# Three hand-written lists of pieces laid out anew, and twelve products without a reader taken out

## The chip, the cores and the metric

One core of a Trainium2 chip runs the whole program. It has five engines with a list of instructions each: PE (matrix products), DVE and ACT (element-wise work), POOL (element-wise work and gathers) and SP (issues transfers). Each engine works through its list in order and waits on semaphores for the others. The metric is the device time of one execution in microseconds (us), lower is better; the figure of a kernel is the median of its runs.

## The reference

Every one of the 8192 tokens (16 sequences of 512, D = 512 features) gets six modulated copies of itself, a two-layer network over their concatenation, a layer norm and a residual:

```python
h = _ln(x, pw_g[pathway_ids], pw_b[pathway_ids])          # 500 rows to choose from
h = _ln(h, cp_g[compartment_ids], cp_b[compartment_ids])  # 5 rows
t = _ln(x, tm_g[time_steps], tm_b[time_steps])
m = x + _mlp_ln(memory_state, ...)[:, None, :]            # n, r alike, from the other states
s = _ln(x, ms_g[scale_type], ms_b[scale_type])
w = softmax(aw)
cat = concatenate([w[0]*h, w[1]*t, w[2]*m, w[3]*n, w[4]*r, w[5]*s], axis=-1)
y = silu(cat @ W1 + b1) @ W2 + b2                          # W1: 3072 x 512, W2: 512 x 512
return x + _ln(y, int_g, int_be)
```

## The kernel before

The branches t, m, n, r and s are linear in x or in the normalised x once the choice of rows is known, so the kernel sorts the tokens by that choice and folds the tables into weights. Three products of 512 x 512 are left for layer 1 of a token: X (the token itself times `wx_`), V (the normalised token times `vs`, a matrix per group of tokens, rebuilt on ACT and DVE when the group changes: pieces `sp` and `bd`, in an If) and H (the h branch times `wh_`). A row gathered per token (`add`) brings what does not depend on x.

The sorted tokens are worked on in 16 tiles of 512 tokens, each of four blocks of 128. Tiles overlap: while tile c is in layer 1, tile p = c-1 is in layer 2 and at its output, tile n = c+1 is being normalised and transposed, and tile m = c+2 is gathered.

The order of all work is written out by hand, in three lists of short names, called pieces. `ORDER` is the head (tables, the sort, all of tile 0 in layer 1 and the front of tile 1), `WINDOW` is run for tiles 0 to 14, and `LAST` for tile 15 and the end. A piece in a list issues its instructions on its engine when the list comes to it, so the list sets the order on each engine, and, for what one piece reads and another writes, who waits for whom. A name is a kind, a tile (a number, or p, c, n, m) and a block or half.

The pieces that this document speaks of:

- In the head: `ax` (PE turns `at_n`, L1025 and L980, for the gathers' index), `xt`, `xv`, `vt`, `vv` (PE transposes a block, ACT copies it into cX or cV, L1117 and L1123), `xs`, `xe`, `xm` (statistics of x), `wu` (`awake`, L401: products of a weight with itself into a bank whose result nobody reads).
- Layer 1: `lX`, `lV`, `lH` are eight products each of 512 columns (L392). From tile 1 on, X and H are done for pairs of blocks by seven half-size products instead of eight, `m7.c.half.1` to `.7` (L440), which accumulate into the banks `u_0`, `u_1` and `p1`. DVE makes their sums of tokens (`u1` to `u4`, L421 to L427) and adds `u` into the rows: `r1` (L449), `r2` (L451), `r5` (L453 and L454), `r3` (L457). `m7.c.0.6` goes into `u_0`, which `r5.c.0` reads.
- Between the layers: `ha`, `hs`, `tz` (add, silu, transpose on DVE and ACT), and `sZ`, `sH`, `sV`, `sX`: SP's transfers that spread the transposed blocks into cZ, cH, cV, cX (four of 64 KB each).
- Layer 2 in the same seven-product way: `q7.p.half.1` to `.7` (L541 and L543) into the banks `pq_0a`, `pq_0b`, `pq_1a`, `pq_1b`; POOL makes the sums (`zs`, L520 to L526). The banks are read by `kf` (ACT copies, L552 and L554), `ku` (ACT, L565), `sf` (DVE, L559 and L561) and `sl` (DVE, L570 and L572) into yb. `q7.p.1.5` and `q7.p.1.7` go into the two halves of `pq_1b`; `kf.p.3` reads the first half, `sf.p.3` the second.
- The end of a tile: `lv`, `lp`, `lb` (L629 and L630) and `po` (POOL scatters the output, L634). The front of the next: `tv` (DVE transposes xm, L190), `f1` (L335 and L336), `f2`, `fv` (L357), `th`.
- In `LAST`: `l2` is the plain layer 2 of tile 15, `la`, `yg`, `ft` (L603, L580, L599) its end on DVE.

Of the kernel before, what the change touches and what calls it, by code (L numbers as in the profile page):

```python
# [44 lines left out]


WINDOW = """
    ha.p.2 lV.c.1 hs.p.2 sh.c.1 tz.p.3 gc.c.2 tz.p.2 sp.c.3 gc.c.3 f1.c.2 fs.c.2 f1.c.3 m7.c.1.1 m7.c.0.1 lV.c.0
    xs.n.0 fs.c.3 sh.c.0 bd.c.3 lV.c.3 fv.c.2 f2.c.2 f2.c.3 sZ.p.2 ga.c.0 sZ.p.0 xs.n.1 q7.p.1.1 fp.c.2 fv.c.3 fn.c.2
    q7.p.0.1 sZ.p.1 fp.c.3 q7.p.0.2 fn.c.3 sZ.p.3 sp.c.2 th.c.2 th.c.3 xs.n.2 zs.p.0 zs.p.1 bd.c.2 q7.p.0.5 kf.p.0  # L50
    q7.p.1.2 sH.c.0 sf.p.0 gh.n.0 zs.p.2 tx.n.3 kf.p.1 tx.n.0 q7.p.0.6 xs.n.3 zs.p.4 q7.p.0.7 ku.p.0 zs.p.5 q7.p.1.5
    zs.p.3 xe.n kf.p.2 tx.n.1 xp.n ga.c.1 sf.p.1 sH.c.3 tx.n.2 xm.n kf.p.3 q7.p.0.3 q7.p.1.7 sf.p.2 nv.n.3 q7.p.0.4
    sl.p.0 zs.p.6 nv.n.1 ga.c.2 zs.p.7 sh.c.3 tv.n.3 tv.n.1 r1.c.0 gc.n.0 sf.p.3 sl.p.1 nv.n.2 tv.n.2 m7.c.0.2 nv.n.0
    ga.c.3 sH.c.2 sH.c.1 lq.p.0 gh.n.1 tv.n.0 q7.p.1.3 lq.p.1 q7.p.1.6 ku.p.1 f1.n.0 q7.p.1.4 sl.p.2 fs.n.0 sl.p.3
    lV.c.2 lq.p.2 u1.c.0 u1.c.1 lq.p.3 va.n u3.c.0 sV.n.0 sV.n.3 u2.c.0 lv.p m7.c.0.4 r1.c.1 m7.c.0.5 lp.p m7.c.1.5
    u2.c.1 fv.n.0 lb.p.1 lb.p.0 vd.n r5.c.0 gc.n.1 u4.c.0 m7.c.0.6 u3.c.1 r5.c.1 gx.m.1 lb.p.2 sp.n.1 po.p.0 r2.c.0
    sV.n.2 f1.n.1 fp.n.0 m7.c.1.6 sV.n.1 sX.n.2 sX.n.0 m7.c.0.7 gx.m.2 sX.n.3 fs.n.1 sp.n.0 r2.c.1 f2.n.0 lb.p.3
    po.p.1 fv.n.1 gx.m.0 gx.m.3 fn.n.0 po.p.2 fp.n.1 bd.n.0 bd.n.1 f2.n.1 m7.c.1.7 m7.c.1.2 fn.n.1 u4.c.1 m7.c.0.3
    r3.c.0 th.n.0 gh.n.2 sh.c.2 ha.c.0 ha.c.1 r3.c.1 hs.c.1 m7.c.1.4 th.n.1 gh.n.3 hs.c.0 tz.c.1 ha.c.3 hs.c.3 po.p.3
    tz.c.0 sX.n.1 m7.c.1.3  # L60
"""
# [15 lines left out]


# [1402 lines left out]
```

## Time and profile before

| | |
|---|---|
| median of 3 runs | 938.56 us (936.71 to 940.25) |
| profiled execution, its span | 935.9 us |
| PE busy | 909.9 us, 97% of the span |
| DVE busy | 745.0 us, 80% |
| POOL busy | 655.0 us, 70% |
| ACT busy | 502.1 us, 54% |

The profile is of one execution. Its time is the span, 935.9 us, and what lies around it; against the median of the runs 2.7 us lie around it. Rows of instructions give the start, the duration, engine, line, operation, the tile written and read, the shapes and a count, and in brackets how long the engine was idle before and what ended that. A duration holds the latency of the pipeline, so instructions on one engine overlap in the rows; from start to start is what one costs the engine.

### The profile page before, as it was taken

How to read it: one execution, taken by the hardware profiler on the slowest of the kernel's cores; microseconds unless marked ns; L12 is line 12 of the kernel's file. 1: busy time of each engine (PE TensorE's matmuls, PEld its weight loads, DVE VectorE, ACT ScalarE, POOL GpSimd, SP SyncE). 2: the span in 40 equal slices, each digit the busy share in tenths (PEclk: the TensorE clock that was granted, in tenths of full speed). 3: DMA queues.
4: the chain of work that ended last, by engine and by line, in shares of the span. 5: the costliest groups of instructions: out<-in, count | busy, mean ns of one | idle time of the engine just before them, and what ended most of it. 6: DMA issues, size and time to landing. Idle time of an engine off the chain costs nothing. (4 is left out here: it accounts for less than half of the span.)

```text
span 935.9 us, 13631 instructions
## 1 busy us (share of the span) xinstructions
PE 909.9 (97%) x3711; PEld 649.5 (69%) x3711; DVE 745.0 (80%) x1359; ACT 502.1 (54%) x1211; POOL 655.0 (70%) x705
## 2 busy tenths in 40 slices
...
GB/s 277 256 183 192 181 226 196 185 238 167 247 170 237 189 209 208 194 207 201 237 181 250 165 240 176 219 208 209 204 195 214 201 234 164 247 166 180 185 46 99
DMA packets 88861, 186.68 MB, mean 199 GB/s; under 512 B 24372, under 2 KB 24372, under 8 KB 88780
## 3 DMA queue, kind: packets, MB, share of 16 engines
...
q14 instruction: 50, 0.41, 0.1%
q10 hardware_dynamic: 704, 0.08, 0.1%
...
## 5 line engine op out<-in xcount | busy, mean ns | idle before, releaser
L392 PE MATMUL p<-vs,cV 128*128 128x512 f32 x504 | 226.3, 596 | 4.0 <-ACTq L237 2.3
L392 PEld LDWEIGHTS p<-vs,cV 128*128 128x128 f32 x504 | 95.9, 191 | 108.5 <-issue 89.5
L339 ACT ACTIVATE junk<-pw 128x512 bf16<-128x512 f32 x60 | 37.7, 629 | 175.2 <-DVE pw L336 84.9
L440 PE MATMUL p<-wh__80,cH 128*128 128x256 f32 x480 | 111.1, 379 | 0.0
L164 POOL DMA_INDIRECT xbs<-in_x,tok x64 | 69.2, 1081 | 44.4 <-DVE yb L630 24.7
L440 PEld LDWEIGHTS p<-wh__80,cH 128*128 128x128 f32 x480 | 91.2, 190 | 12.4
L634 POOL DMA_INDIRECT out<-yb,tok x64 | 65.4, 1023 | 41.8 <-issue 29.2
L164 POOL DMA_INDIRECT pw<-in_pw,i_pw x64 | 64.7, 1010 | 39.0 <-DVE rH L190 19.9
L164 POOL DMA_INDIRECT cp<-cp_rows,i_cp x64 | 78.8, 1231 | 17.5 <-issue 12.2
L380 POOL TENSOR_TENSOR xbs<-xbs,rows 128x512 f32<-128x512 f32 x64 | 82.2, 1286 | 1.2
L164 POOL DMA_INDIRECT add<-rows,i_add x64 | 67.0, 1048 | 14.7 <-issue 12.5
L361 POOL TENSOR_TENSOR rsh<-veh,mhalf 128x1 f32<-128x1 f32 x64 | 49.2, 768 | 37.2 <-DVE veh L357 32.4
L365 ACT ACTIVATE pw<-pw,rsh 128x512 f32<-128x512 f32 x64 | 44.8, 717 | 53.8 <-issue 23.7
L463 ACT ACTIVATE add<-add 128x512 f32<-128x512 f32 x64 | 38.5, 626 | 63.8 <-DVE add L460 45.4
L335 DVE SCALAR_TENSOR_TENSOR pw<-xbs,sums,pw 128x512 f32<-128x512 f32 x60 | 53.6, 893 | 18.5 <-DMA pw<-in_pw,i_pw 16.2
L372 DVE SCALAR_TENSOR_TENSOR pw<-pw,sumsh,cp 128x512 f32<-128x512 f32 x60 | 44.5, 748 | 18.7 <-DMA cp<-cp_rows,i_cp 7.8
L190 DVE STREAM_TRANSPOSE rH<-pw 128x512 f32<-128x512 f32 x60 | 41.3, 703 | 20.5 <-ACT pw L365 19.8
L440 PE MATMUL p<-wt,cH 128*128 128x256 f32 x240 | 56.7, 379 | 0.0
L440 PE MATMUL u<-wt,ss 128*128 128x256 f32 x240 | 54.5, 380 | 0.4 <-DVE add L454 0.4
L440 PE MATMUL u<-wt,cX 128*128 128x256 f32 x240 | 54.4, 380 | 0.0
L440 PEld LDWEIGHTS u<-wx__79,cX 128*128 128x128 f32 x240 | 45.6, 190 | 12.6 <-issue 5.0
L440 PE MATMUL u<-wx__79,cX 128*128 128x256 f32 x240 | 54.2, 379 | 0.0
...
## 6 DMA issues: line engine op xcount, KB each, us to landing
cZ<-rZ SPq DMA_DIRECT2D x256, 64.0 KB
...
```

The source lines that it names most:

```text
L164: nc.gpsimd.indirect_dma_start(dst, None, table, bass.IndirectOffsetOnAxis(ap=idx, axis=0), **kw)
L190: nc.vector.transpose(rot[:, :, :, j, :].rearrange("p q c t -> p c q t"), src.rearrange("p (c q t) -> p c q t", c=NC, q=Q))
L335: nc.vector.scalar_tensor_tensor(h, st["xb"][:, j, :], st["sums"][:, 1, j : j + 1], h, ALU.add, ALU.mult)
L339: nc.scalar.activation(junk, x, AF.Identity, accum_out=sums[:, 0, k : k + 1])
L361: nc.gpsimd.tensor_tensor(rs, st.pop(("ve", j)), mhalf[:, :1], ALU.pow)
L365: nc.scalar.mul(pw[:, :D], pw[:, :D], st.pop(("rs", j)))
L372: nc.vector.scalar_tensor_tensor(pw[:, :D], pw[:, :D], st["sh", j][:, 1], cp, ALU.add, ALU.mult)
L380: nc.gpsimd.tensor_add(st["xb"][:, j, :], st["xb"][:, j, :], rows[:, 2, :])
L392: nc.tensor.matmul(st["p1", g], st["c" + blk][:, g, c, :], m[:, c, :], start=(blk == first and c == 0), stop=(blk == last and c == NC - 1) ...
L440: nc.tensor.matmul(dst, m[:, c], at_["half1"][k][:, c], start=(k == 1 and c == 0), stop=(c == NC - 1), skip_group_check=True)
L463: nc.scalar.activation(st["add", g], st["add", g], AF.Silu)
L634: nc.gpsimd.indirect_dma_start(out_rows[j], bass.IndirectOffsetOnAxis(ap=tok[:, j, w : w + 1], axis=0), yb[:, j, :], None)
```

## The change

The text of the three lists is new, and nothing else. From `ORDER` the twelve `wu` pieces are gone; the function `awake` stays, without a caller. All other pieces are the same, in another order: on every engine in the head, in the steady groups and in the last group.

```diff
 ORDER = """
-    wk.1.2 h2.1 fx dk lt pk bx sz wk.1.1 by kd wu.lX.0.1.0 xs.0.0 xt.0.0 tk tt wk.1.3 wk.2.1 gx.e0.0 xv.0.0
-    wu.lX.0.1.8 lw fg lo xs.0.1 fl.2 wm.4 h2.2 gx.e0.1 wu.lX.0.1.1 fl.1 scl he.1 xt.0.1 ax he.2 gx.e0.3 gx.e0.2 ac
...
+    se lw lo lt wk.1.0 wk.1.2 fx bx dk wk.1.3 wk.1.1 wk.2.1 by kd tk fg h2.1 ax cv xt.0.1 xv.0.1 he.1 fl.2 tt
+    xs.0.1 pwi gx.e0.0 gh.0.2 gx.e0.1 gh.0.0 xs.0.3 xs.0.2 xs.0.0 xe.0 wk.2.2 xp.0 xt.0.0 h2.2 h2.0 cg xm.0 he.0
...
 WINDOW = """
...
-    zs.p.3 xe.n kf.p.2 tx.n.1 xp.n ga.c.1 sf.p.1 sH.c.3 tx.n.2 xm.n kf.p.3 q7.p.0.3 q7.p.1.7 sf.p.2 nv.n.3 q7.p.0.4
...
+    sl.p.0 nv.n.3 kf.p.3 nv.n.1 q7.p.1.7 q7.p.0.4 zs.p.7 tv.n.3 sf.p.3 tv.n.1 sl.p.1 sH.c.0 sH.c.2 sH.c.1 sH.c.3
+    q7.p.1.6 q7.p.1.4 q7.p.1.3 lV.c.2 nv.n.2 nv.n.0 lq.p.0 ku.p.1 f1.n.0 sl.p.2 tv.n.2 sl.p.3 f1.n.1 lq.p.1 fs.n.0
```

What stands on the engines at three places. A row is a line, an operation, the tile written and read with its number, the shape, and a count where it repeats.

The first is PE in the head, around the transposes of `ax` (tile `pa`). Before:

```order
L401 MATMUL awake_lX_0_1_563<-wt_82 128x512
L1117 MATMUL ptX1_635<-ident_93,xbs2_90 128x128 x4
L1025 MATMUL pa_640<-ident_93,room1_115 128x64
L980 MATMUL pa_640<-at_n_285,ident_93 32x16 x16
L1129 MATMUL po0_681<-xbs1_89,room1_115 32x512 x4
L1099 MATMUL pdr_686<-tg_122,picks_199 34x512
L401 MATMUL awake_ex_4_688<-wt_82 128x512
```

Now:

```order
L1048 MATMUL pnx_520<-b_at_290,room1_115 64x7 x4
L1048 MATMUL pnx_520<-b_at_290,g_at_291 64x7 x8
L1129 MATMUL po1_558<-xbs0_88,room1_115 32x512 x4
L1025 MATMUL pa_563<-ident_93,room1_115 128x64
L980 MATMUL pa_563<-at_n_285,ident_93 32x16 x16
L1188 MATMUL pv_581<-ident_93,vr_278 128x9 x4
L1117 MATMUL ptX1_586<-ident_93,xbs2_90 128x128 x4
```

The products into `awake` are gone, and `pa` stands ahead of the transposes of x (`ptX`), behind the first `po`.

The second is PE in a steady group, in layer 2 of tile 5, around the bank `pq5_1b`. Before:

```order
L541 LDWEIGHTS ident_93
L541 MATMUL pq5_1b_3794<-b2r_104,ident_93 128x256
L543 MATMUL pq5_1b_3794<-w2_81,cZ5_3779 128x256 x2
L543 MATMUL pq5_0b_3804<-w2_81,yb_91 128x256 x2
L543 MATMUL pq5_1b_3794<-w2t_1432,zs5_3862 128x256 x2
L543 MATMUL pq5_0b_3804<-w2t_1432,cZ5_3779 128x256 x2
L440 MATMUL p1_6_0_3751<-wh__80,cH6_3844 128x256 x4
L543 MATMUL pq5_1b_3794<-w2_81,zs5_3862 128x256 x2
```

Now:

```order
L543 MATMUL pq5_0b_3782<-w2_81,yb_91 128x256 x2
L541 LDWEIGHTS ident_93
L541 MATMUL pq5_1b_3849<-b2r_104,ident_93 128x256
L543 MATMUL pq5_1b_3849<-w2_81,cZ5_3772 128x256 x2
L543 MATMUL pq5_1b_3849<-w2t_1407,zs5_3863 128x256 x2
L543 MATMUL pq5_0b_3782<-w2t_1407,cZ5_3772 128x256 x2
L543 MATMUL pq5_1a_3848<-w2t_1407,zs5_3863 128x256 x2
L543 MATMUL pq5_1b_3849<-w2t_1407,cZ5_3772 128x256 x2
```

The product into `pq5_0b` that stood between the first two products into `pq5_1b` now stands ahead of both.

The third is DVE in the same group, from the front of tile 6 to `r5` of tile 5. The first part, before:

```order
L335 SCALAR_TENSOR_TENSOR pw6_0_3412<-xbs2_90,sums_3318,pw6_0_3412 128x512
L336 SCALAR_TENSOR_TENSOR pw6_0_3412<-pw6_0_3412,rsx_3438 128x512
L570 TENSOR_TENSOR yb_91<-yb_91 128x256
L572 TENSOR_TENSOR yb_91<-yb_91,pq4_1b_3356 128x512
L237 UNCONDITIONAL_BRANCH
L421 TENSOR_TENSOR ss5_3522<-cX5_3179,cH5_3406 128x512 x2
L425 TENSOR_TENSOR cX5_3179<-cX5_3179 128x512
L423 TENSOR_TENSOR ss5_3522<-ss5_3522,cX5_3179 128x512
L616 TENSOR_SCALAR vey_3546<-ssy_3495 128x4
L449 TENSOR_TENSOR add5_2_3464<-add5_2_3464,u5_1_3303 128x256
L423 TENSOR_TENSOR ss5_3522<-ss5_3522,cX5_3179 128x512
```

Now:

```order
L190 STREAM_TRANSPOSE rV6_3463<-xm6_2_3496 128x4x4x32
L572 TENSOR_TENSOR yb_91<-yb_91,pq4_1b_3411 128x512
L335 SCALAR_TENSOR_TENSOR pw6_1_3435<-xbs2_90,sums_3288,pw6_1_3435 128x512
L336 SCALAR_TENSOR_TENSOR pw6_1_3435<-pw6_1_3435,rsx_3433 128x512
L237 UNCONDITIONAL_BRANCH
L421 TENSOR_TENSOR ss5_3526<-cX5_3244,cH5_3468 128x512 x2
L616 TENSOR_SCALAR vey_3529<-ssy_3500 128x4
L190 STREAM_TRANSPOSE rV6_3463<-xm6_0_3498 128x4x4x32
L423 TENSOR_TENSOR ss5_3526<-ss5_3526,cX5_3244 128x512
L449 TENSOR_TENSOR add5_2_3547<-add5_2_3547,u5_1_3302 128x256
L357 TENSOR_SCALAR veh_3558<-sumsh_3511 128x1
L427 TENSOR_TENSOR cH5_3468<-cH5_3468,ss5_3526 128x512
```

The second pair of `f1` (tile `pw6_1`) now stands ahead of the sums of tokens, and a transpose of `xm6` and the sum into cH (L427) among them. The end of the stretch, before:

```order
L629 SCALAR_TENSOR_TENSOR yb_91<-yb_91,rsy_3557,rows_92 128x512
L630 TENSOR_TENSOR yb_91<-yb_91,xbs0_88 128x512
L228 TENSOR_LOAD new_v_106
L453 TENSOR_TENSOR add5_0_3346<-add5_0_3346,u5_0_3308 128x256
L454 TENSOR_TENSOR add5_1_3440<-add5_1_3440,u5_0_3308 128x256
L427 TENSOR_TENSOR cH5_3406<-cH5_3406,ss5_3522 128x512
L425 TENSOR_TENSOR cX5_3179<-cX5_3179 128x512
```

Now:

```order
L629 SCALAR_TENSOR_TENSOR yb_91<-yb_91,rsy_3553,rows_92 128x512
L630 TENSOR_TENSOR yb_91<-yb_91,xbs0_88 128x512
L425 TENSOR_TENSOR cX5_3244<-cX5_3244 128x512
L453 TENSOR_TENSOR add5_2_3547<-add5_2_3547,u5_1_3302 128x256
L454 TENSOR_TENSOR add5_3_3551<-add5_3_3551,u5_1_3302 128x256
L453 TENSOR_TENSOR add5_0_3330<-add5_0_3330,u5_0_3312 128x256
L454 TENSOR_TENSOR add5_1_3555<-add5_1_3555,u5_0_3312 128x256
```

The pair that adds `u5_1` stood behind the pair that adds `u5_0` and the sums of tokens after it, and now stands ahead of that pair; a sum of tokens (L425) that stood further up now follows the two `lb`.

More of the change, by code (lines that the diff above doesn't have):

```diff
@@ new lines @@
+    f2.0.2 cn fl.1 cw ct vt.0.3 xt.0.3 vt.0.2 fl.0 ca wk.2.0 cm xs.e0.3 fn.0.2 xe.e0 pk gr.e0.1 xp.e0 xm.e0 nv.0.0
+    nv.e0.1 vv.0.3 scl ht.0.2 vt.0.0 f2.0.0 mt.e0.1 wk.2.3 cr gx.e1.2 gr.e0.0 ey.1 gh.0.1 rp.0 xs.e1.1 xv.0.3
+    xv.0.2 va.1 nv.e0.0 nv.e0.3 xs.e1.0 vv.0.0 lX.0.1 fv.0.0 ar mt.e0.0 f1.0.1 fs.0.1 xa ey.0 rp.1 fp.0.0 gx.1.0
+    gc.0.1 gx.1.3 fn.0.0 ez.0 nv.e0.2 rc.0 xs.e1.2 wl.4 rc.1 sp.0.1 vv.0.2 ez.1 ro.0 ro.1 ht.0.0 ex.0 lX.0.2
+    lX.0.3 f2.0.1 bd.0.1 hv.0.0 fv.0.1 xe.e1 gx.1.2 gr.e0.2 gr.e0.3 ea.0 gh.0.3 gx.1.1 xp.e1 mt.e0.2 mt.e0.3 ee.0
@@ new lines @@
+    xm.e1 vd.0 ey.2 ey.3 gc.0.3 gr.e1.2 fp.0.1 xs.1.2 xs.1.3 wh sp.0.0 va.0 ez.3 nv.e1.2 xs.1.0 fn.0.1 xs.1.1 ez.2
+    eo.0 f1.0.3 fs.0.3 mt.e1.2 tx.1.0 f2.0.3 fv.0.3 hv.0.2 tx.1.2 xe.1 ex.1 lV.0.1 ey.6 lX.0.0 ht.0.1 sh.0.2 ea.3
+    ea.2 ea.1 fp.0.3 gr.e1.0 xp.1 gh.1.3 fn.0.3 ez.6 wm.0 sp.0.3 nv.e1.0 wm.1 nv.e1.1 wm.2 ht.0.3 ex.3 gr.e1.1
+    gh.1.2 ea.6 bd.0.0 tx.1.3 bd.0.3 hv.0.1 mt.e1.1 xm.1 mt.e1.0 ee.3 tx.1.1 ee.1 lV.0.0 ex.6 ey.4 ey.5 wm.3 ez.5
+    nv.1.1 sp.0.2 ez.4 nv.1.2 wl.1 f1.1.3 bd.0.2 tv.1.1 ee.6 f1.1.2 eo.3 eo.1 eo.6 ex.2 ex.5 ex.4 lV.0.2 lV.0.3
@@ new lines @@
+    gc.1.2 gc.1.3 ea.4 ea.5 sp.1.0 fs.1.3 nv.1.3 sp.1.1 fs.1.2 ee.5 ee.2 vd.1 tv.1.3 bd.1.0 hv.0.3 fv.1.3 fv.1.2
+    f2.1.3 f2.1.2 fp.1.3 fp.1.2 nv.1.0 fn.1.3 wl.0 wl.2 fn.1.2 wl.3 bd.1.1 ee.4 th.1.3 th.1.2 wq tv.1.2 tv.1.0
+    gc.1.0 sh.0.0 gh.1.1 gh.1.0 eo.5 eo.2 lH.0.0 lH.0.3 sX.1.0 gc.1.1 sp.1.3 gx.2.0 eo.4 wb lH.0.2 f1.1.0 f1.1.1
+    lH.0.1 sX.1.3 sX.1.1 sX.1.2 sV.1.1 sV.1.3 sV.1.0 sV.1.2 ga.0.2 gx.2.1 ga.0.0 ga.0.3 ga.0.1 sh.0.3 sh.1.1
+    ha.0.0 ha.0.2 ha.0.3 fs.1.0 fs.1.1 hs.0.2 hs.0.0 sp.1.2 hs.0.3 bd.1.3 tz.0.2 bd.1.2 tz.0.3 fv.1.0 fv.1.1
@@ L56 @@
[L56 to L60, printed above, removed]
+    ha.p.2 lV.c.1 gc.c.2 gc.c.3 f1.c.2 tz.p.3 sp.c.3 hs.p.2 tz.p.2 fs.c.2 xs.n.0 f1.c.3 fv.c.2 f2.c.2 bd.c.3
@@ new lines @@
+    bd.c.3 fv.c.3 bd.c.2 f2.c.3 f2.c.2 sZ.p.1 sZ.p.0 m7.c.1.1 lV.c.3 lV.c.2 m7.c.0.1 q7.p.0.1 fp.c.2 fp.c.3 ga.c.3
+    ga.c.2 zs.p.0 zs.p.1 zs.p.2 zs.p.3 ga.c.0 fn.c.3 fn.c.2 kf.p.0 th.c.3 th.c.2 q7.p.0.5 q7.p.0.6 q7.p.0.7 kf.p.1
+    ku.p.0 sH.c.2 sH.c.0 sH.c.1 sH.c.3 sZ.p.3 sZ.p.2 sf.p.1 q7.p.0.2 q7.p.0.4 m7.c.1.2 q7.p.0.3 m7.c.0.2 m7.c.0.4
+    sl.p.0 r1.c.0 sf.p.0 sl.p.1 r1.c.1 u1.c.0 u2.c.0 u1.c.1 lq.p.0 lq.p.1 u2.c.1 u4.c.0 vr.p.1 u3.c.1 u3.c.0
+    vr.p.0 u4.c.1 m7.c.0.5 m7.c.1.5 m7.c.1.6 m7.c.0.6 m7.c.1.3 pr.p.1 ga.c.1 pr.p.0 zs.p.4 zs.p.5 sh.c.0 zs.p.6
```

61 lines of the change are left out of this document (22 added, 39 removed).

## Prediction

> **What bounds the kernel now.** I read the busy shares first, then the stretches, then the chain of PE's waits, last the order of time on PE and DVE inside one steady group.
>
> ```profile
> PE 909.9 (97%) x3711; PEld 649.5 (69%) x3711; DVE 745.0 (80%) x1359; ACT 502.1 (54%) x1211; POOL 655.0 (70%) x705
> ```
>
> PE is the bound: 97% busy, DVE 80%. The table of stretches (length, busy time of PE, PEld, DVE, ACT, POOL, then the granted clock) says where PE's few idle microseconds lie: in the head, and not in a steady group.
>
> ```profile
> 37.23:47.47 10.24, 10.24 (x56) 6.22 (x55) 7.56 (x28) 2.24 (x10) 4.27 (x5) 0.50 0.68 232
> 47.47:80.07 32.60, 29.76 (x186) 12.39 (x186) 18.00 (x57) 20.82 (x48) 19.24 (x19) 1.00 0.56 186
> 80.07:143.24 63.17, 61.59 (x161) 27.95 (x159) 48.24 (x89) 44.25 (x94) 43.42 (x43) 1.00 0.69 203
> ...
> 146.46:149.87 3.41, 3.41 (x5) 1.35 (x4) 1.05 (x2) 0.00 (x0) 2.64 (x4) 0.50 0.95 266
> ```
> ```profile
> 303.17:353.79 50.62, 50.62 (x206) 38.07 (x205) 40.40 (x73) 26.75 (x66) 37.71 (x38) 1.00 0.74 206
> 710.78:762.49 51.71, 50.92 (x206) 37.98 (x205) 44.21 (x78) 29.65 (x71) 37.89 (x40) 1.00 0.72 203
> 151.32:814.26 662.94, 660.05 (x2654) 493.50 (x2653) 550.37 (x974) 361.37 (x879) 489.28 (x489) 1.00 0.73 206
> ```
>
> A steady group takes 50.62 us, and PE works through all of it; DVE has 10 us to spare over the group, but that average says nothing about one place in the list. From the same product of one group to that of the next, 13 groups take 662.94 us, 4.9 over 13 x 50.62; the group of 710.78 alone has 1.1 of that (PE idle 0.8), and in all 13 PE is idle for 2.9. PE's waits, in total, number and longest:
>
> ```profile
> PE p L392 <- ACTq L237: 2.3, 1, 2.3
> ...
> PE pq_0a L543 <- DVE yb L559: 1.0, 1, 1.0
> ...
> PE pq_1b L543 <- DVE yb L561: 0.7, 1, 0.7
> PE pq_0b L543 <- POOL cZ L522: 0.4, 1, 0.4
> ...
> PE u L440 <- DVE add L454: 0.4, 1, 0.4
> ```
>
> So whatever order is better can win a few microseconds in the steady groups, and whatever order is worse is paid 14 times.
>
> **The head.** Removed: the 12 products without a reader. They stand on PE, but what counts is what stood behind them: `ax`, PE's transposes for the index of the gathers, is now the fourth piece. ACT's waits up to the last copy into cX, which the first product of layer 1 (80.07 us) needs:
>
> ```profile
> 54.64 0.21 ACT L1039 COPY at_n<-pa 128x64 f32<-128x64 f32 x1 [4.11 <-PE awake_ex L401]
> ...
> 66.55 0.81 ACT L306 ACTIVATE xm<-xbs,nmx,rsx 128x512 f32<-128x512 f32 x1 [2.40 <-issue]
> 70.10 0.59 ACT L1227 COPY br<-pb 128x512 f32<-128x512 f32 x1 [2.74 <-PE pb L1222]
> ...
> 76.49 0.59 ACT L1258 COPY rows<-pr 120x512 f32<-120x512 f32 x1 [1.84 <-DVE six L1003]
> ...
> 78.55 0.61 ACT L1123 COPY cX<-ptX 128x512 f32<-128x512 f32 x1
> ```
>
> The four waits sum to 11.1 us: the most that can be won ahead of that copy; the least is nothing, if other waits take their place. I take 7, nearer the upper end, since the 4.11 goes for certain and pieces that ACT needs (xm, f1) move ahead of what it waits for. Layer 1 of tile 0 is then 63.17 us of nearly full PE, the same products; of the 7 I let 2 be lost to gathers on POOL, whose list has no idle to give. At 143.24 PE waited 2.3 us for ACT's branch at L237, which stood behind a silu; the branch (`sp.1.2`) now comes two pieces earlier, and with the wait goes the half clock of 146.46 to 149.87, worth half of 3.41, 1.7. Together 7 - 2 + 2.3 + 1.7 = 9 us won, between 2 and 13.
>
> [...] By the clock of 1.00 that the rows give for the stretches after 47.47, I leave the sum at -9.
>
> **Steady group, first place: q7 into pq_1b.** In the order before, another product (q7.0.3, into pq_0b) stood between q7.1.5 and q7.1.7. Now these two are neighbours. q7.1.7 writes the bank from which ACT copies the result of q7.1.5 (L554), and waits for that copy. PE and ACT in the group of 249 us, then the same three in the last group, where before, too, the copy ended last:
>
> ```profile
> 269.46 1.10 PE L543 MATMUL pq_1b<-w,cZ 128*128 128x256 f32 x4
> 270.40 1.03 PE L543 MATMUL pq_0b<-w,yb 128*128 128x256 f32 x4
> 271.27 1.03 PE L543 MATMUL pq_1b<-w2t,zs 128*128 128x256 f32 x4
> 272.13 1.03 PE L543 MATMUL pq_0b<-w2t,cZ 128*128 128x256 f32 x4
> ...
> 277.31 3.60 PE L392 MATMUL p<-vs,cV 128*128 128x512 f32 x8
> ...
> 285.92 1.24 PE L440 MATMUL u<-wt,ss 128*128 128x256 f32 x5
> ```
> ```profile
> 270.65 0.37 ACT L554 COPY yb<-pq_1b 128x256 f32<-128x256 f32 x1 [1.17 <-POOL rsx L289]
> ```
> ```profile
> 908.73 1.13 PE L543 MATMUL pq_1b<-w,cZ 128*128 128x256 f32 x4 [0.44 <-POOL cZ L522]
> ...
> 910.23 0.37 ACT L554 COPY yb<-pq_1b 128x256 f32<-128x256 f32 x1 [1.63 <-PE pq_1b L543]
> ...
> 910.65 0.73 PEld L543 LDWEIGHTS pq_1b<-w2t,zs 128*128 128x128 f32 x4 [0.33 <-ACT yb L554]
> 910.65 1.13 PE L543 MATMUL pq_1b<-w2t,zs 128*128 128x256 f32 x4
> ```
>
> Issue of q7.1.5 ends at 270.40, the copy ends at 271.02: with nothing between, PE stalls 271.02 - 270.40 = 0.62 and a little for the signal. In the last group the stretch from the four products' end (908.73 + 0.97 = 909.70) to q7.1.7 is 0.95. I take 0.65, with 0.95 as upper end; the lower is 0, if PE doesn't wait for a copy of the other half of the bank. [...]
>
> **Steady group, second place: r5 ahead of m7.0.6.** m7.0.6 writes u_0 and waits until DVE's r5.0 (L453, L454) has read it. DVE's list from sf.3, which needs q7.1.7, to the end of r5.0, in the group of before:
>
> ```profile
> 273.41 0.41 DVE L561 TENSOR_TENSOR yb<-yb,pq_1b 128x256 f32<-128x256 f32 x1
> ...
> 274.34 1.29 DVE L190 STREAM_TRANSPOSE rV<-xm 128x512 f32<-128x512 f32 x2
> 275.55 0.71 DVE L335 SCALAR_TENSOR_TENSOR pw<-xbs,sums,pw 128x512 f32<-128x512 f32 x1
> ...
> 277.05 0.43 DVE L570 TENSOR_TENSOR yb<-yb 128x256 f32<-128x256 f32 x1
> ...
> 281.92 0.75 DVE L629 SCALAR_TENSOR_TENSOR yb<-yb,rsy,rows 128x512 f32<-128x512 f32 x1 [0.18 <-POOL rsy L621]
> ...
> 284.71 0.41 DVE L453 TENSOR_TENSOR add<-add,u 128x256 f32<-128x256 f32 x1
> ...
> 285.37 0.68 DVE L427 TENSOR_TENSOR cH<-cH,ss 128x512 f32<-128x512 f32 x1
> 285.97 0.68 DVE L425 TENSOR_TENSOR cX<-cX 128x512 f32<-128x512 f32 x1
> ```
>
> Before: 285.37 - 273.41 = 11.96, of which 0.18 a wait, so 11.78 of work, and PE's m7.0.6 (285.92) came 0.55 later: no stall. Now the same stretch also holds, start to start, f1.n.1 (277.05 - 275.55 = 1.50), a third transpose tv (0.60), u4.1 (285.97 - 285.37 = 0.60) and r5.1 (0.66, as r5.0): 15.14. sf.3 can't begin before q7.1.7 is done, 0.27 after its issue (the row of 271.27: 1.03 long, next issue after 0.86; 0.1 for the signal). On PE, from the end of issue of q7.1.7 to m7.0.6, stand the same pieces in number: four q7, one lV, four m7, 285.92 - 272.13 = 13.79. Stall: 0.27 + 15.14 - 13.79 = 1.62, whatever slack DVE brought into the group, since both ends of the chain hang on q7.1.7. I take 1.65; it could be 1.0 if DVE's operations run shorter beside less traffic, and 2.2 if a wait (a root, a copy) falls into the chain. What is queued behind r5.0 on DVE (u3.1, lb.1, r2.0) is late by as much, but its readers (m7.0.7) have three PE pieces of 1.73 before them.
>
> The group becomes 50.62 + 0.65 + 1.65 = 52.9. Fourteen of them cost 32 us (14 x 1.4 = 20 to 14 x 3.15 = 44). The later PE also hides some of the 4.9 us above 13 x 50.62: -3 (0 to -5).
>
> **Costed at nothing.** SP's spreads: sZ.p.0 and 1 now go first, which is what q7.0 needs first; sH and sV come later by at most one spread set, behind PE's older work. POOL: sh.c.3 and the gathers for two groups on end its list; it is busy 37.7 of 50.62, and if its cover went, each shift would cost about 1.3. ACT's nv.n.3 ahead of the copy: its input is there before.
>
> **The end.** DVE's chain behind the last product of layer 2 took, before:
>
> ```profile
> 928.18 0.69 DVE L603 TENSOR_TENSOR yb<-p,rows 128x512 f32<-128x512 f32 x1
> ...
> 930.24 0.75 DVE L599 SCALAR_TENSOR_TENSOR yb<-yg,sd,xbs 128x512 f32<-128x512 f32 x1
> ```
>
> 2.81 us; now two blocks' scale and sum stand behind it, some 1.7 more (two operations of 0.61 and 0.66, and a root). The last group's waits above (0.7, 0.4 and their like on pq_1b) mostly go: 1.5 back. Net 0, within 1.5.
>
> **Sum.** Profiled execution 935.9; -9 + 32 - 3 + 0 gives 955.9. The median of the runs, 938.56, is 2.7 above it: 958.6, so 958.
>
> **Rivals.**
> 1. *Neither steady wait is real* (DVE reaches r5.0 in time, the copy doesn't hold q7.1.7); then only the head shows: 938.6 - 9 = 930 (926 to 936), faster. For it: DVE has 10 us spare per group and before had no stall at either place. Against: the chain hangs on q7.1.7 at both ends, so spare time elsewhere can't be spent in it. It decides if the chain is under 13.5 us.
> 2. *One of the two:* 14 x 0.65 or 14 x 1.65 alone, less 9 and 3: 936 to 950.
> 3. *Cold head.* Without the twelve products PE stays at 0.50 in the sparse head. Priced by the half clock of 146.46: layer 1's opening costs 1.7 to 3.4 more and the transposes ahead of it 2 to 3: +5, with both waits 963. That clock of 1.00 after 47.47 came with the products, so the trace can't exclude it. [...]
> 4. *The reorder does nothing:* steady groups at 50.6 and ACT's head waits replaced by others: 936 to 941.
>
> **Chances.** Both waits with a warm head 0.54, with a cold head 0.18, one wait 0.13, rival 1 0.10, rival 4 0.05. Likeliest: 958, its own range 947 to 967. The range 932 to 968 leaves out most of rival 1 and the tails. 0.5% is 4.7 us, about what these runs (936.71 to 940.25) can tell from no change: faster 0.12 (rival 1 and an end of rival 2), same 0.08, slower 0.80.
>
> **What would show it.** After: a steady period of 52.9 on PE; among PE's waits, `u L440 <- DVE add L454` some 14 times at 1.6 and `pq_1b L543 <- ACT yb L554` some 14 times at 0.65; no L401 rows; the first layer 1 product near 73; no 0.50 clock near 140. A period of 50.6 with neither wait makes the prediction wrong; so does a new wait elsewhere, a product that waits for a spread above all.

## Result and the profile after

The changed kernel is slower by 12%: 1050.39 us (1048.23 to 1055.6, 4 runs) against 937.63 us (935.19 to 940.25, 4 runs) beside it, a ratio of 1.1196 with a 95% interval of 1.1154 to 1.1238. The forecast was 958, with a range of 932 to 968: the sign was right, the size was not. The profiled execution has a span of 1046.4 us, 110.5 more than before. Its busy shares, in the order of the page (busy time, share, instructions):

```profile
PE 937.7 (90%) x3687; PEld 663.5 (63%) x3687; DVE 740.4 (71%) x1359; ACT 499.0 (48%) x1211; POOL 648.6 (62%) x705
```

PE, with its weight loads (PEld), is the only engine with more busy time (909.9 and 649.5 before), although it has 24 instructions fewer: some of its work ran at half clock (0.50 in the last row below). The stretches (length, busy time of PE, PEld, DVE, ACT, POOL, granted clock, share of the DMA engines, GB/s): a whole steady group of the changed kernel, and the piece of it behind its longest wait.

```profile
438.84:498.67 59.83, 54.61 (x205) 39.91 (x204) 41.16 (x74) 26.62 (x66) 37.75 (x39) 0.94 0.62 176
...
478.26:484.49 6.23, 6.22 (x15) 4.97 (x16) 3.17 (x6) 0.72 (x1) 3.95 (x6) 0.50 0.30 106
```

The 205 products that took 50.62 us of a full PE now take 59.83: 5.2 us idle, and 54.61 busy instead of 50.62. The period, here and below the mean distance from the first product into `pq_0a` of one group to that of the next over 13 groups, is 59.01 (51.00 before). PE's waits after:

```profile
PE u L440 <- DVE add L454: 47.7, 14, 4.7
PE p L440 <- DVE cH L427: 16.5, 14, 1.2
...
PE pq_1b L543 <- issue: 5.9, 7, 1.2
PE p L392 <- DVEq L237: 3.8, 1, 3.8
PE pq_1b L543 <- ACT yb L554: 3.7, 5, 1.2
PE pq_1b L543 <- POOL cZ L522: 2.4, 2, 2.2
```

The two waits of the prediction are there, `u L440 <- DVE add L454` in 14 groups and `pq_1b` (put down to the copy, to issue or to others) in about as many. The second has the forecast size or somewhat more, 0.5 to 1.2 in most groups; the first is 3.31 in 13 groups, and 4.65 in the last, where 1.62 was forecast. A third wait, for cH, was not forecast at all. By parts of the span: the first product into u of tile 1 comes at 144.80 instead of 151.32, 6.5 us earlier; between tile 1 and the start of the last group the 14 groups lose 114.6; the last group and the end take 2.4 more.

Why 3.31: DVE and PE in the group at 456 us, in order of time (start, duration, then the instruction, in brackets the idle time before and what ended it).

```profile
459.56 0.42 DVE L561 TENSOR_TENSOR yb<-yb,pq_1b 128x256 f32<-128x256 f32 x1 [0.40 <-issue]
...
466.71 1.29 DVE L421 TENSOR_TENSOR ss<-cX,cH 128x512 f32<-128x512 f32 x2 [1.11 <-DMA cH<-rH]
...
468.62 0.65 DVE L423 TENSOR_TENSOR ss<-ss,cX 128x512 f32<-128x512 f32 x1
471.82 0.42 DVE L449 TENSOR_TENSOR add<-add,u 128x256 f32<-128x256 f32 x1 [2.55 <-PE u L440]
...
472.22 0.68 DVE L427 TENSOR_TENSOR cH<-cH,ss 128x512 f32<-128x512 f32 x1
...
477.80 0.41 DVE L454 TENSOR_TENSOR add<-add,u 128x256 f32<-128x256 f32 x1
```
```profile
468.06 3.72 PE L440 MATMUL u<-wx__79,ss 128*128 128x256 f32 x16
472.96 1.99 PE L440 MATMUL p<-wh__80,cH 128*128 128x256 f32 x8 [1.18 <-DVE cH L427]
478.26 6.78 PE L440 MATMUL u<-wt,ss 128*128 128x256 f32 x16 [3.31 <-DVE add L454]
```

DVE stands idle for 2.55 us in the middle of the chain: r1.c.1 (L449) waits for PE's products into u, which end at about 471.7. These are m7.c.0.5 and m7.c.1.5. r1.c.1 needs m7.c.1.1 only, some 30 us older; but in the new list it is written behind m7.c.1.5, which goes into the other half of the same bank, and so it waits for it. In the list before it stood ahead, and ran while the same products were still to come (r1.c.1 on DVE, then m7.c.0.5 and m7.c.1.5 on PE, before):

```profile
280.67 0.41 DVE L449 TENSOR_TENSOR add<-add,u 128x256 f32<-128x256 f32 x1
...
282.47 3.62 PE L440 MATMUL u<-wx__79,ss 128*128 128x256 f32 x16
```

What follows on DVE up to r5.c.0 takes 6.4 us (471.82 to 478.2), and PE has only m7.c.1.3 to do in that time. The sixteen matmuls behind the wait then take 6.78 us for what took 3.62 before: the half clock.

### The profile page after: what moved, and what is told of

The parts are those of the page before. It is cut to its first block, busy times and chain, and to the rows that moved or that the text cites. A ratio compares the mean times of both kernels' runs of the same rounds, so it can differ in the third digit from the quotient of the medians.

```text
span 1046.4 us, 13670 instructions
## 1 busy us (share of the span) xinstructions
PE 937.7 (90%) x3687; PEld 663.5 (63%) x3687; DVE 740.4 (71%) x1359; ACT 499.0 (48%) x1211; POOL 648.6 (62%) x705
## 4 chain that ended last, share of the span: by engine, by line
PE 51%; SPq 13%; DVE 11%; DMA 4%; issue 4%; POOL 2%; ACT 1%; POOLq 0%; DVEq 0%; ACTq 0%
PE u L440 20%; SPq L198 13%; PE p L392 11%; PE p L440 8%; PE pq_1b L543 4%; PE pq_0b L543 3%; DMA cX<-rX 2%; PE pq_1a L543 2%; DVE yb L630 2%; PE pq_0a L543 2%; DVE yb L629 2%; DMA cH<-rH 2%; DVE add L454 1%; DVE add L453 1%; DVE cX L425 1%
## 5 line engine op out<-in xcount | busy, mean ns | idle before, releaser
L392 PE MATMUL p<-vs,cV 128*128 128x512 f32 x512 | 231.4, 596 | 3.8 <-DVEq L237 3.8
L392 PEld LDWEIGHTS p<-vs,cV 128*128 128x128 f32 x512 | 97.8, 191 | 103.4 <-issue 93.2
L440 PE MATMUL p<-wh__80,cH 128*128 128x256 f32 x480 | 114.8, 382 | 16.5 <-DVE cH L427 16.5
L440 PE MATMUL u<-wt,ss 128*128 128x256 f32 x240 | 83.7, 525 | 47.7 <-DVE add L454 47.7
L440 PEld LDWEIGHTS p<-wh__80,cH 128*128 128x128 f32 x480 | 90.0, 190 | 39.7 <-DVE cH L427 22.1
L440 PEld LDWEIGHTS u<-wt,ss 128*128 128x128 f32 x240 | 64.3, 274 | 67.0 <-DVE add L454 53.3
L164 POOL DMA_INDIRECT add<-rows,i_add x64 | 76.1, 1189 | 21.0 <-issue 15.0
L164 POOL DMA_INDIRECT xbs<-in_x,tok x64 | 65.9, 1030 | 23.7 <-issue 16.0
L164 POOL DMA_INDIRECT cp<-cp_rows,i_cp x64 | 63.9, 998 | 18.9 <-issue 14.2
L460 DVE TENSOR_TENSOR add<-p,add 128x512 f32<-128x512 f32 x64 | 43.6, 682 | 41.5 <-PE p L440 21.6
L306 ACT ACTIVATE xm<-xbs,nmx,rsx 128x512 f32<-128x512 f32 x64 | 51.7, 812 | 31.7 <-DVE nmx L300 17.0
L440 PEld LDWEIGHTS u<-wx__79,cX 128*128 128x128 f32 x240 | 45.6, 190 | 19.0 <-issue 12.9
L440 PE MATMUL u<-wx__79,cX 128*128 128x256 f32 x240 | 56.7, 379 | 0.0
L440 PE MATMUL u<-wx__79,ss 128*128 128x256 f32 x240 | 54.7, 381 | 1.3 <-DVE ss L421 1.3
L440 PE MATMUL p<-wt,cH 128*128 128x256 f32 x240 | 54.4, 379 | 0.0
L440 PE MATMUL u<-wt,cX 128*128 128x256 f32 x240 | 54.2, 379 | 0.0
```

What stands on the lines that cost most here:

```text
L164: nc.gpsimd.indirect_dma_start(dst, None, table, bass.IndirectOffsetOnAxis(ap=idx, axis=0), **kw)
L306: nc.scalar.activation(t, st["xb"][:, j, :], AF.Identity, bias=st["nm"][:, j : j + 1], scale=st["rs"][:, j : j + 1])
L392: nc.tensor.matmul(st["p1", g], st["c" + blk][:, g, c, :], m[:, c, :], start=(blk == first and c == 0), stop=(blk == last and c == NC - 1) ...
L440: nc.tensor.matmul(dst, m[:, c], at_["half1"][k][:, c], start=(k == 1 and c == 0), stop=(c == NC - 1), skip_group_check=True)
L460: nc.vector.tensor_add(st["add", g], st["p1", g], st["add", g])
```

## Experiments

Each kernel is described by the names that are moved; the difference shown is that of the list, cut to the place (`...`). In e1, e3 to e5, e7, e8, e10 to e12, e15 and e16 lines stand two lower in the rows than above, in e6 and e9 mostly four higher.

**e1: r1 listed early in the changed kernel.**

```diff
 WINDOW (changed)
-    ... m7.c.1.2 m7.c.0.5 m7.c.1.5 gc.n.1 ga.c.2 gc.n.0 ga.c.3 lp.p ga.c.1 r1.c.1
+    ... m7.c.1.2 m7.c.0.5 gc.n.1 ga.c.2 gc.n.0 ga.c.3 lp.p ga.c.1 r1.c.1 m7.c.1.5
```

> The changed kernel, with one name moved in WINDOW: m7.c.1.5 behind r1.c.1. Every engine keeps its order; only r1.c.1 no longer comes, in the program, behind a product into the same bank. Theory A (r1's add into the rows waits for m7.c.1.5 because it was listed behind it, and the sums and r5 behind it on DVE start from there): the wait of 1.2 for cH (L427) goes, the wait of m7.c.0.6 for r5 (L454) shrinks from 3.3 to the 1.6 to 2.6 that the chain from sf.3 gives, no half clock in the steady groups, period 53 to 54.5 instead of 59.0, time 968 to 985. Theory B (DVE is simply too full there, the listing does not matter): the waits and the time stay, 1040 to 1056.

986.63 us (ratio to before 1.0517, 1.0462 to 1.0571), period 54.83. The order on every engine is the same as in the changed kernel, and 64 of the 113 us are gone.

```profile
PE u L438 <- DVE add L452: 24.5, 14, 2.9
```

The wait for cH is gone, the wait for r5 is down from 47.7 to 24.5, 1.75 a group; the clock over the groups is 0.99. It is theory A, though 1.6 us above its time and 0.3 above its period. What is left against before, 49 us, is taken up in e5, e10 and e15.

**e2: r1 listed late in the kernel before.**

```diff
 WINDOW (before)
-    ... lv.p m7.c.0.4 r1.c.1 m7.c.0.5 lp.p m7.c.1.5
+    ... lv.p m7.c.0.4 m7.c.0.5 lp.p m7.c.1.5 r1.c.1
```

> The kernel before, with one name moved in WINDOW: r1.c.1 behind m7.c.1.5. The order on every engine stays. Theory A: r1.c.1 waits for the end of m7.c.1.5; then r1, u2, fv, two lb and r5.c.0 (0.33+0.6+0.1+2.8+0.66 = 4.5 us) run before m7.c.0.6 may start, a wait of 4.6 to 4.9 in each of 14 groups. That alone is 14 x 4.8 = 67 us, time 1005; with the half clock after each such wait, 3.4 to 6.8 us at 0.5, another 24 to 45 us, time 1030 to 1050. Theory B (the listing does not matter): 938, no such wait.

1035.84 us (1.1041, 1.0981 to 1.1102), period 57.98. One name moved behind three others, no engine's order changed, and 97 us are lost:

```profile
PE u L440 <- DVE add L454: 60.0, 13, 4.6
PE u L440 <- DVE add L453: 4.6, 1, 4.6
...
160.00:900.00 740.00, 676.36 (x2598) 504.86 (x2598) 545.22 (x957) 354.11 (x863) 472.15 (x482) 0.94 0.64 180
```

4.6 us in each of 14 groups, as worked out, and a mean clock of 0.94 over the groups (1.00 before). 4.61 of the 7.0 us by which the group is longer (57.98 against 51.0) is the wait; the rest goes with the half clock, granted once in each of the 14 groups.

**e3 and e7: the changed head alone.** `ORDER` of the changed kernel, `WINDOW` and `LAST` of before; e7 is the same kernel once more, in a single run, although its label speaks of a spread.

> The kernel before with the changed ORDER alone (no products without a reader, head laid out anew); WINDOW and LAST as before. Theory A: the head's gain shows, 6.5 us at the first product of tile 1: 931 to 933, period 50.6 and no wait for L454. Theory B (the head leaves the engines in another state and the groups pay it back): 936 to 945.

> The kernel of e3 again, once, beside the next one, for its profile: 930 to 936.

933.06 us (0.9934, 0.9901 to 0.9967), and 931.95 in e7. The head wins 6 us, with the period of before (51.05). It is the fastest kernel of this study, together with e16 and e8, from which the spread of the runs does not part it.

**e8: only the twelve products taken out.** All twelve `wu` pieces deleted from `ORDER` of before.

> The kernel before without its twelve products without a reader, all else in the order of before. Theory A (they hold up the transposes of ax and the work behind them): the first product of layer 1 comes up to 4 us earlier, time 934 to 938. Theory B (without them the clock stays at 0.50 up to about 75 us): 940 to 946.

934.89 us (0.9943, 0.9919 to 0.9967): theory A. Most of what the new head wins comes with the deletion alone. Ahead of layer 1 there is more half clock than before, 17.1 us in three stretches against 10.2 in one (mean clock of the execution 0.986, before 0.990), but not up to 75 us, and it costs less than the products did.

**e4 and e11: the DVE list mended by hand.** e4 has r5.c.0 and r5.c.1 ahead of the two lb, on top of e1 and e5; e11 also has u3.c.0 ahead of both and r2 ahead of lb.p.2 and lb.p.1.

```diff
 WINDOW, DVE (e4)
-    fv.n.0 u4.c.1 lb.p.0 u2.c.0 lb.p.2 u3.c.0 r5.c.1 r5.c.0
+    fv.n.0 u4.c.1 u2.c.0 r5.c.0 r5.c.1 lb.p.0 lb.p.2 u3.c.0
```

> The changed kernel with names moved in WINDOW at three places: r1.c.1 ahead of m7.c.1.5; q7.p.1.7 ahead of kf.p.3 (so ACT's copy waits for the product, not the product for the copy); r5.c.0 and r5.c.1 ahead of the two lb on DVE, u2.c.0 with them. Theory A: all three waits go (L427 1.2, L454 3.3, pq_1b 0.9), clock 1.00, period 50.6 to 51.5, time 932 to 946. Theory B (the new order is limited by DVE as a whole or by late spreads of cH): period above 53, time above 965.

> The kernel of e4 (1017.9), with u3.c.0 and r2.c.0, r2.c.1 ahead of two of the lb on DVE, so that m7.c.0.7 and m7.c.1.7 no longer wait for r2 behind three lb. Theory C (the loop through m7.c.1.7, SP and cH sets the period): the loop is 33 us of SP, 2.3 of landing, 1.3 of u1 and 13.8 of PE from m7.0.5 to m7.1.7, 50.4, so PE's own 50.6 to 52 again, time 934 to 955. Theory B (this DVE order loses as much elsewhere): above 970.

1017.9 us (1.0833) and 1020.76 us (1.0927): theory A fails for e4 and theory C for e11, and both times lie in the range of theory B. The waits named are mostly gone, and others stand in their place; e4, then e11:

```profile
PE u L438 <- DVE add L449: 30.1, 15, 2.4
PE p L390 <- DVEq L235: 11.3, 7, 4.7
...
PE u L438 <- DVE add L452: 6.5, 10, 2.0
```
```profile
PE p L438 <- DVE cH L425: 22.7, 14, 4.0
PE p L390 <- ACT junk L337: 13.6, 7, 2.4
PE p L390 <- DVE vs L252: 7.6, 3, 3.2
```

r2, then u4 and the rebuilds come too late instead. Moving the piece that is waited for makes the next one late; the list is not mended at one place.

**e5: the copy of pq_1b listed late.**

```diff
 WINDOW (e1)
-    ... sl.p.0 nv.n.3 kf.p.3 nv.n.1 q7.p.1.7
+    ... sl.p.0 nv.n.3 q7.p.1.7 kf.p.3 nv.n.1
```

> The kernel of e1 (986.6) with one more name moved: q7.p.1.7 ahead of kf.p.3 and nv.n.1. Every engine keeps its order; ACT's copy of pq_1b now waits for the product instead of the product for the copy. Theory A (each wait of q7.1.7 is on PE's path by itself, as the prediction had it): the 0.7 us a group goes, 14 x 0.7 = 10, time 976 (973 to 979). Theory B (the wait only moved PE back to where DVE's chain holds it anyway): m7.c.0.6 waits as much longer, 983 to 988.

986.66 us, as e1: theory B. The wait for the copy is gone (of the waits into pq_1b, 15 us in e1, 6.5 for a sum on POOL are left in 4 groups) and the period is nearly the same (54.54), since another chain holds the group; the wait for r5 rose from 24.5 to 28.8, the one for u1 from 3.1 to 7.5.

**e6 and e9: products put into the gap.** 14, then 7, products of 256 columns on PE, ahead of m7.c.0.6, into pq_1b after its last reader.

> The changed kernel with 14 products of 256 columns put on PE ahead of m7.c.0.6, 14 x 0.216 = 3.0 us, into a bank of layer 2 that has been read out (pq_1b); nobody reads them. They fill most of the 3.3 us for which PE waits there. Theory A (that idle time is what brings the half clock, and the half clock costs 1.7 to 3.1 in most groups): the wait stays as PE's path, but the clock is 1.00 through the groups and the period falls from 59.0 to about 56.5, time 1010 to 1025. Theory B (the half clock comes from something else, or costs nothing): clock at 0.50 as often, time 1045 to 1060.

> As e6, with 7 products instead of 14: in e6 each took two passes, 0.43 us and not 0.216, so the filler was 6.05 us and overran the wait by 2.7. Seven are 3.0 us and fit into the wait of 3.3. Theory A (idle time brings the half clock, which costs about 2.4 us in a mean group): clock 1.00 in the groups, period 56.4 to 56.8, time 1012 to 1022. Theory B (the half clock costs PE nothing that the loop around it would not cost anyway): period 58 to 59, time 1040 to 1052.

In e6 each product stood as two matmuls in the trace and took 0.43 us, so the filler of 6.05 us overran the wait by 2.7; 1060.3 us, period 59.39: theory A in the clock, at half in the groups only once, at 943 us, theory B in the time. Without the overrun the period would be 56.7, an estimate. In e9 seven fit: 1027.84 us (1.1003, 1.0968 to 1.1038), period 57.42 against 59.01, between the two theories. The product behind r5 starts as late as before, 10.1 us after m7.c.0.5 (10.2 in the changed kernel); only the time ahead of it is filled:

```profile
410.20 3.19 PE L404 MATMUL pq_1b<-wt 128*128 128x256 f32 x14
413.67 3.72 PE L444 MATMUL u<-wt,ss 128*128 128x256 f32 x16 [0.28 <-DVE add L458]
```

Over the groups:

```profile
160.00:900.00 740.00, 704.54 (x2813) 524.16 (x2812) 541.75 (x967) 357.25 (x872) 476.76 (x487) 1.00 0.65 184
```

The clock is 1.00 where the changed kernel has 0.96 over the same stretch. So the idle time brings the half clock, and extra work that nobody reads makes the kernel 2% faster. The 1.6 us a group that it wins is less than the 2.4 expected: two groups still have a stretch of half clock and take 61.15 and 60.45.

**e10: the products that read cX early.** m7.c.1.3 and m7.c.0.2 behind m7.c.1.7 on PE, on top of e5. m7.c.0.2 then reads cH after u4.c.0 has written it, so this kernel computes another product there.

> The kernel of e5 (986.7) with m7.c.1.3 and m7.c.0.2 behind m7.c.0.7 and m7.c.1.7 on PE; the other engines keep their order. Theory C (the group's length is a loop: the last product that reads cX, m7.c.1.7, frees the buffer for sX of the next tile; SP then issues sX, sZ, sH one after the other, 32 us; cH's landing starts u1, the sums, r5 and m7.0.6 up to m7.1.7 again): m7.1.7 comes one product pair earlier, 1.73 us, and the period falls by that, time 960 to 967. Theory B (PE waits for DVE's r5 and nothing hangs on m7.1.7): the wait of m7.0.6 grows by what was put behind it, period as in e5, 983 to 990.

1022.78 us (1.0949): neither theory's number. The wait for r5 grew by the 1.73 that was put behind it (2.12 to 3.84), as theory B says, and with 3.2 to 5.0 us of idle time there the half clock came back in all 14 groups (mean clock of the execution 0.951, in e5 0.983), which neither had. The run does not decide on the loop.

**e15: one spread more.** `sX.n.3` issued twice, on top of e5.

> The kernel of e5 (986.7) with one spread issued twice: four more transfers of 64 KB into block 3 of cX, the same data, behind sX of the next tile; 4 x 0.65 = 2.6 us of SP's queue in each group. Theory C (a loop through m7.c.1.7, SP's sX, sZ and sH, and u1 sets the period): the period grows by 2 to 3, time 1012 to 1030. Theory B (DVE's list sets it; SP has 6 us idle ahead of sV and 6 ahead of sX in each group): 985 to 990.

1035.49 us (1.1022, 1.0967 to 1.1077), period 58.29 against 54.54: 3.75 us for 2.6 us more of SP's queue. That is theory C in kind, 5 us above its range; a queue with idle time in each group that nothing hung on would have cost nothing. More half clock came with it: e15 has twelve stretches in its groups, e5 two. And part of the cost comes in by another door than cH: sZ stands behind sX too, and PE now waits 18.2 us in 13 groups for a sum of cZ (`pq_0b L541 <- POOL cZ L520`; 0.6 in e5). SP and PE in e5 show the loop:

```profile
575.14 10.99 SPq L196 DMA_DIRECT2D cX<-rX  x16
586.24 10.03 SPq L196 DMA_DIRECT2D cZ<-rZ  x16
596.38 10.78 SPq L196 DMA_DIRECT2D cH<-rH  x16
613.10 10.02 SPq L196 DMA_DIRECT2D cV<-rV  x16
628.90 11.19 SPq L196 DMA_DIRECT2D cX<-rX  x16
```
```profile
571.49 3.62 PE L438 MATMUL u<-wt,cX 128*128 128x256 f32 x16
574.95 1.89 PE L438 MATMUL p<-wh__80,cH 128*128 128x256 f32 x8
...
612.40 3.72 PE L438 MATMUL u<-wx__79,ss 128*128 128x256 f32 x16 [0.65 <-DVE ss L419]
...
619.97 3.72 PE L438 MATMUL u<-wt,ss 128*128 128x256 f32 x16 [2.12 <-DVE add L452]
```

SP starts sX at 575.14, 0.2 after PE's last product on the old cX (issue ends 574.95), and issues sX, sZ and sH with nothing between until 607.16. cH lands, DVE forms u1, PE goes on at 612.40, waits for r5, and frees cX again before 628.90, one period of 53.76 later. Before, SP's wait for PE is on other products, and PE is full.

**e12 and e16: SP's spreads at the end of the head in PE's order.** On top of e3.

```diff
 ORDER (changed)
-    sX.1.0 ... eo.4 ... sX.1.3 sX.1.1 sX.1.2 sV.1.1 sV.1.3 sV.1.0 sV.1.2
+    sX.1.0 ... eo.4 ... sV.1.1 sX.1.2 sV.1.0 sV.1.3 sX.1.3 sX.1.1 sV.1.2   (e16; in e12 all seven ahead of eo.4)
```

> The kernel of e3 (changed head, steady and last groups of before), with SP's spreads at the end of the head in the order in which PE reads them: sX.1.0, sV.1.1, sX.1.2, sV.1.0, sV.1.3, then the rest; before, all four sX went ahead of sV. Theory A (the wait of 4.1 us for cV at the first product of tile 1 is SP's queue): the wait goes, and the half clock behind it; 4 to 7 us below e3, 926 to 930. Theory B (the head is bound by DVE's or ACT's work behind it): 931 to 935.

> As e12 (the kernel of e3 with SP's spreads at the end of the head in PE's order), but with the transfer eo.4 left ahead of them: in e12 it stood behind 22 us of spreads, and the gathers that read what it writes were late. Theory A (then only SP's order is changed): the wait for cV at the first product of tile 1 shrinks from 4.1 to what ha leaves, 1 to 3 us; time 927 to 932. Theory B (no gain over e3): 931 to 935.

e12: 946.94 us (1.0138), outside both theories. The transfer eo.4 stood behind 22 us of spreads, gathers read what it writes, and PE waited 18.1 us behind them. e16: 933.41 us (0.9935, 0.9911 to 0.9959), no better than e3: theory B. The wait of 4 us is still there, now for cX instead of cV.

**e13: neighbours in pq_1b, in the kernel before.** q7.p.0.3 ahead of q7.p.1.5. It then also stands ahead of the sum that it reads (zs.p.3), so it multiplies older data.

> The kernel before with one name moved in WINDOW: q7.p.0.3 ahead of q7.p.1.5, so that q7.p.1.5 and q7.p.1.7 are neighbours on PE. Nothing else moves. The prediction's first term alone: PE waits 0.62 to 0.95 for ACT's copy in each of 14 groups, 9 to 13 us, time 944 to 952 (by the median of before in these runs, 935 to 939, plus 9 to 13). Rival: the wait is hidden, 935 to 940.

956.56 us (1.0172, 1.0131 to 1.0212), above both forecasts; period 52.4, 52.02 in most groups:

```profile
PE pq_1b L543 <- POOL zs L526: 7.4, 14, 0.6
PE pq_1b L543 <- ACT yb L554: 7.1, 14, 0.5
```

```profile
273.45 1.03 PE L543 MATMUL pq_1b<-w,cZ 128*128 128x256 f32 x4
274.98 1.13 PE L543 MATMUL pq_1b<-w2t,zs 128*128 128x256 f32 x4 [0.51 <-ACT yb L554]
...
279.23 1.13 PE L543 MATMUL pq_1b<-w,zs 128*128 128x256 f32 x4 [0.53 <-POOL zs L526]
```

The copy is waited for 14 times, 0.51 in the rows. From start to start the step is 1.53 (274.98 - 273.45) where four such matmuls without a wait take 0.86, so the copy costs 0.67 a group, the prediction's 0.65. The period of most groups rises by 1.40. The other 0.7 is a later sum on POOL, and comes of the edit: zs.p.3 now stands behind the product that reads it, POOL waits 2.07 us for that product (`yb L526 <- PE pq_0b L543`, at 273.58), and the sum that q7.p.1.6 needs is late by it.

**e14 and e17: a longer chain ahead of r5, in the kernel before.**

```diff
 WINDOW, DVE (before)
-    lb.p.1 lb.p.0 vd.n r5.c.0 u4.c.0 u3.c.1 r5.c.1 lb.p.2 r2.c.0 f1.n.1 r2.c.1 f2.n.0 lb.p.3
+    lb.p.1 lb.p.0 vd.n lb.p.2 lb.p.3 u3.c.1 r5.c.0 u4.c.0 r5.c.1 r2.c.0 f1.n.1 r2.c.1 f2.n.0      (e17)
```

> The kernel before with f1.n.1, lb.p.2 and u3.c.1 moved ahead of r5.c.0 on DVE (1.50 + 1.40 + 0.60 = 3.5 us), so that the chain from sf.p.3 to the end of r5.c.0 is 0.27 + 11.96 + 3.5 = 15.7, as in the prediction's second term, against 13.79 on PE. By that arithmetic m7.c.0.6 waits 1.5 to 1.9 in each of 14 groups, clock 1.00, 21 to 27 us: 957 to 966. Rival (a wait of this kind brings the half clock or a longer loop with it): period above 53, time above 975.

> The kernel before with lb.p.2, lb.p.3 and u3.c.1 moved ahead of r5.c.0 on DVE (1.40 + 1.40 + 0.60 = 3.4 us), none of which waits for a gather. The prediction's second term alone: 0.27 + 11.78 + 3.4 - 13.79 = 1.66, with the wait of 0.18 for a root 1.84, in each of 14 groups; period 52.3 to 52.6, clock 1.00, time 23 to 27 us above before, 961 to 967. Rival: DVE stays as late at sf.p.3 as it was, the wait is 285.37 + 3.4 - 285.92 = 2.9, period 53.5 and more, time 978 or above.

e14 is spoiled: f1.n.1 stood ahead of the landing of its gathered row (DVE idle 88 us for `pw<-in_pw`), 1073.85 us. e17 is clean, 997.34 us (1.0648, 1.0611 to 1.0685), and the arithmetic of the prediction fails in it. The wait is 2.8 in each group, the rival's number, not 1.66 to 1.84:

```profile
505.16 1.03 PE L543 MATMUL pq_1b<-w2t,zs 128*128 128x256 f32 x4
...
507.30 0.41 DVE L561 TENSOR_TENSOR yb<-yb,pq_1b 128x256 f32<-128x256 f32 x1
```

sf.p.3 starts 2.14 after q7.p.1.7, exactly as in the kernel before (273.41 - 271.27), although PE now leaves DVE 2.8 us more in each group. DVE's lateness there is not a leftover that a slower PE lets it work off; it hangs on PE too, on products further up (its row on pq_0a, L559, starts 2.3 us after the product into pq_0a in both kernels, and from there to sf.p.3 it takes 7.1 and 7.2). And 2.8 us of idle time bring the half clock in 11 of 14 groups (mean clock 0.97 over 160 to 900 us, 1.00 before); the period is 55.5, not the 53.8 that the wait alone would give.

## Why the prediction was wrong

- **The head, -9:** right in kind, 6.5 in the trace and 6 in e3, but not by the path forecast, so the nearness is partly luck. The 4.11 us wait of ACT's copy of `pa` is gone, yet that copy comes at 57.13, later than before (54.64). The first product of layer 1 comes at 70.26, 9.8 us earlier where 7 was forecast, and 3.3 of these are lost again ahead of tile 1: PE still waits 3.8 us at its first product (`p L392 <- DVEq L237`; 2.3 before) and the half clock still follows (0.50 for 3.41 us from 139.74), where the prediction had both gone. What won the 9.8, beyond the deletion (e8), stays open.
- **First steady term, 0.65 a group:** the wait and its size are right, 0.5 to 1.2 in the trace and 0.67 on its own in e13. The upper end, 0.95, was misread: in the last group a product into pq_1a (909.70 to 910.56) stands in that stretch. And e5 shows that the term is not simply added to the rest: taken out of e1 it wins nothing.
- **Second steady term, 1.65 a group:** the place is right; the step that failed is the sum, which took the whole stretch of DVE from sf.p.3 to the end of r5.c.0 as work, 15.14 us, and let only sf.p.3 wait for PE. In the group at 456 us that stretch is 18.57 (459.56 to 478.13): 14.91 of work, as forecast, and two waits. Shorter DVE operations beside less traffic, the forecast's lower end, hardly showed: DVE was busy for 740.4 us at 178 GB/s, before for 745.0 at 199. u1 waits 1.11 for the landing of cH (7 of 14 groups have such a wait). r1.c.1 waits 2.55 (42.1 in all 14 groups) for m7.c.1.5, since it is listed behind it and reads the same bank; the chain starts anew there, 6.4 us before m7.c.0.6 may go, with 1.7 us of PE work to cover it. That made 3.31 of 1.62 and brought the wait of 1.18 for cH. e1 and e2 show the part of r1 from both sides. The prediction let q7.p.1.7 wait for a copy of the other half of its bank; r1 had a wait of the same kind, worth 64 us in e1 and 97 in e2, and the prediction did not follow it down the DVE list. That e1 then has 1.75 a group, close to the 1.65, is partly luck: its stretch still holds waits for cH (1.45 at 607 us), and e17 shows that the sum does not hold in the kernel before.
- **The range of these two:** its lower end, 14 x 1.4, does not follow from the terms' own lower ends, 0 and 1.0, which give 14 us and not 20. The result lies far off the other end.
- **The clock:** the sum has no term for it in the groups. The waits for r5 bring 3.4 or 6.8 us of half clock in 13 of 14 groups, 61 us at 0.50 in all, so by estimate some 30 us of lost PE time, or 2.2 a group. e9 shows that the idle time is the cause.
- **The loop through SP:** not in the prediction, which costed SP's order at nothing. In the changed lists sX waits for m7.c.1.7, and sX, sZ and sH stand in one row ahead of cH. e15 shows that SP is on the path, through cZ as well as cH; that this loop holds e1 and e5 at 54.5 to 54.8 is read from the trace and not shown, and e10 could not confirm it.
- **The last group, 0:** 2.4 slower, a little beyond the bound of 1.5.
- **The sum by parts:** -6.5 head, +114.6 groups, +2.4 end is the 110.5 of the span. Of the groups' 8.0 us each (59.01 against 51.00), 3.4 is the wait for r5, 1.2 the one for cH, about 1.0 pq_1b, and 2.2, by the estimate above, the clock.
- **The rivals:** of the cold head (third), whose price was an estimate from the one half clock of 146.46, e8 shows the longer half clock but not the cost: that kernel is faster than before. None of the four had a wait that brings the half clock with it.
